# Two selective-scan layers and two token layers on one core: another order of the state loads, other transfers for B, C and delta, one more state buffer

## The chip, the cores and the metric

The kernel runs on one core of a Trainium2 chip. The metric is device time in microseconds; lower is better. Three runs of the kernel before gave 12473.74, 12483.95 and 12504.42 us; their median, 12483.95 us, is what the change is compared with.

## The reference

The input is a batch of four 64 x 64 images with 96 channels. Layers 0 and 1 normalise the image and add the result of a two-dimensional selective scan; layers 2 and 3 are token layers (an attention without softmax and a quantised feed-forward block). The change touches the scan layers alone. In these an image is projected to 192 channels (E), convolved, and read in four directions (K): by rows, by columns, and both backwards. Each direction gives sequences of L = 4096 steps. Cut to what matters:

```python
dts, Bmat, Cmat = split(x_dbl, [R, R + N])          # R = 6, N = 16 states
delta = softplus(dts @ dt_w + bias)                 # per direction and channel
A = -exp(A_logs)
def step(h, inp):                                   # h: batch, direction, channel, 16 states
    u, d, b, c = inp
    h = exp(d * A) * h + d * b * u
    y = sum over the states of h * c
```

So every channel of every direction and image has 16 states that run through 4096 steps. The four directions' y are added, normalised, gated and projected.

## The kernel before

Two images are worked on together, so there are four phases: layer 0 for pairs 0 and 1, layer 1 for pairs 0 and 1 (`Scans.run`). Each phase has a preparation (`prepare`), which writes what the scan needs to DRAM, and a scan stretch (`scan_phase`), followed by a finish that runs beside the next preparation. Last come the token layers.

The 128 partitions of the scan are 4 groups of states (a "quarter" of 32 partitions each) x 8 sequences (G: 4 directions x 2 images) x 4 states. The time axis is cut into 8 chunks (NC) of 512 steps (TC), the channels into 16 blocks (NEB) of 12 (EB). A block of a chunk is a unit; a stretch has 128 units, four stretches 512.

Preparation writes four things to DRAM per chunk: delta, split into three bf16 parts that add up to the fp32 value (NP16 = 3, L323); the product du = delta x u twice, as two copies (L319); and the rows of B and C, 32 for each sequence (bc, L301).

For a unit, SyncE's queue gets these transfers, in the order of `store` and `load`:

- four stores of y of the unit before (L461),
- one load of delta, 24 partitions (3 parts x 8 sequences) of 12 channels x 512 steps in bf16, 12 KB a partition (L376),
- six loads of h, the state tile [128, 12, 512] in fp32, which starts out as du (L396). All 16 states of a sequence start from the same du, so a row of du is read four times for four partitions of a quarter. The two middle quarters (partitions 32 to 95) come by one transfer out of both copies, once for channels 0 to 5 and once for 6 to 11; then quarter 0 (partitions 0 to 31) in two transfers, then quarter 3 (96 to 127) in two.

B and C of a chunk are tiles of 128 partitions; each is loaded by four transfers of 32 partitions (L344). B of the next chunk is asked for after the last scan of block 8, C of the chunk after next after block 15.

On the chip a unit then passes through five engines, in an order written out by hand in `scan_phase`: POOL multiplies h by B in place, three channels at a time (L406); PE replicates delta onto the 128 partitions, adding up its three parts on the way, by a matmul with a 0/1 matrix `rep` on 24 rows (L412); ACT makes exp(A x delta) of it (L416); DVE runs the scan over 512 steps, one instruction per channel (L423); PE contracts the unit before with C over the states (L441), and ACT copies the result out (L453). The weights for the contraction, `cw`, are made by ACT from C (L360), 16 operations for a chunk: the first chunk's ahead of the first decay, the next chunk's in between, from block 2 on.

PE replicates four channels ahead of the scan, ACT decays three ahead, POOL is half a unit ahead. Units 0 to 2 are loaded at the start, with C of chunk 1 behind them; after the last scan of unit `at` the load of unit `at + 3` is issued. h has four buffers, delta three. Every transfer signals one of eight semaphores in turn and waits for the one that used that semaphore before it.

Of the kernel before, what the change touches and what calls it, by code (L numbers as in the profile page):

```python
# [9 lines left out]
F32 = mybir.dt.float32  # L10
F16 = mybir.dt.float16
BF16 = mybir.dt.bfloat16
# [12 lines left out]
NS = 16  # L25
R = 6
K = 4
G = 2 * K
PAD = HW + 2
TC = 512  # L30
NC = L // TC
ROWS = TC // HW
EB = 12
NEB = E // EB
ER = EB // 4
PITCH = 2
NP16 = 3
XD = 2 * NS + R + 1
XD2 = 64 + XD
HID = 384  # L40
# [40 lines left out]
class Consts:  # L81
# [9 lines left out]
        self.eps = pool.tile([128, 1], F32, name="eps")  # L91
        self.nc.vector.memset(self.eps, EPS)

    def scans(self, pool):
        rep = self.load(pool, "rep", [128, 128])
        self.rep = pool.tile([128, 128], BF16, name="rep16")
        self.nc.vector.tensor_copy(self.rep, rep)
        self.perm = self.load(pool, "perm", [128, K, 128])
        self.unit = self.load(pool, "unit", [128, 128])
        self.gmask = self.load(pool, "gmask", [128, G])  # L100
        self.group = self.load(pool, "group", [C, C])
        self.one_row = self.load(pool, "one_row", [XD2, 1])
# [25 lines left out]
class Scans:  # L128
    def __init__(self, tc, ctx, cst, a):
        nc = self.nc = tc.nc  # L130
        self.tc, self.cst, self.a = tc, cst, a

        def pool(name, bufs, **space):
            return ctx.enter_context(tc.tile_pool(name=name, bufs=bufs, **space))

        self.dram = pool("stage", 2, space=DRAM)
        self.keep = pool("keep", 2)
        cst.scans(pool("const_s", 1))

    def bank(self):  # L140
        return self.p_c.tile([128, TC], F32, name="c")
# [6 lines left out]
    def prepare(self, ph):  # L148

        nc, cst, a, pre = self.nc, self.cst, self.a, ph.pre  # L150
        ph.gs = self.keep.tile([C, 2, 2], F32, name="gs", bufs=3)
        ph.delta = [
            self.dram.tile([NP16, G, E, TC], BF16, name="delta", bufs=2 * NC) for _ in range(NC)
        ]


        ph.du = [
            self.dram.tile([2, G, E + PITCH, TC], F32, name="du", bufs=2 * NC) for _ in range(NC)
        ]
        ph.bc = [self.dram.tile([G, 2 * NS, TC], F32, name="bc", bufs=2 * NC) for _ in range(NC)]  # L160
        ph.ud = self.dram.tile([C, 2, HW, 2, 64], F32, name="ud")
        ph.y = self.dram.tile([64, G, 2, 2, NEB, 16 * EB], F32, name="y")
        x = ph.x_in[ph.pair]

        with self.tc.tile_pool(name="prep", bufs=1) as wp, self.tc.tile_pool(
            name="steps", bufs=2
        ) as sp:

            def load(name, shape, at=0):
                t = wp.tile([at + shape[0]] + shape[1:], F32, name=name)  # L170
                nc.sync.dma_start(t[at:], a[pre + name])
                return t

            xp = load("x_proj", [C, 2, 2, XD2])
            dt_w = load("dt_w", [XD2 - 2 * NS, 2, E], at=2 * NS)
            conv_b = load("conv_b", [C, 2])
            ds = load("Ds", [C, 2, K])
            dsum = wp.tile([C, 2], F32, name="dsum")
            nc.vector.tensor_reduce(dsum, ds, mybir.AxisListType.X, ALU.add)
            yield  # L180


            st = wp.tile([C, 2, 8, 6], F32, name="st")
            with self.tc.tile_pool(name="stats", bufs=2) as rp:
                for hl in range(8):
                    raw = rp.tile([C, 8, 2, 64], F32, name="raw")
                    nc.sync.dma_start(raw, x[:, hl * 8 : hl * 8 + 8])
                    for i in range(2):
                        nc.vector.bn_stats(st[:, i, hl], raw[:, :, i])
                    yield  # L190
            for i in range(2):
                mv = wp.tile([C, 2], F32, name="mv")
                nc.vector.bn_aggr(mv, st[:, i].rearrange("p c s -> p (c s)"))
                ps = self.bank()
                nc.tensor.matmul(ps[:C, :1], cst.group, mv[:, 0:1], start=True, stop=True)
                gs = ph.gs[:, i]
                nc.vector.tensor_copy(gs[:, 0:1], ps[:C, :1])
                d = wp.tile([C, 1], F32, name="d")
                nc.vector.tensor_tensor(d, mv[:, 0:1], gs[:, 0:1], ALU.subtract)
                nc.vector.scalar_tensor_tensor(d, d, d, mv[:, 1:2], ALU.mult, ALU.add)  # L200
                ps = self.bank()
                nc.tensor.matmul(ps[:C, :1], cst.group, d, start=True, stop=True)
                ln = wp.tile([C, 2], F32, name="ln")
                neg_rsqrt(nc, cst, ps[:C, :1], ln[:, 0:1], gs[:, 1:2], ln[:, 1:2])
                nc.vector.tensor_scalar_mul(gs[:, 1:2], gs[:, 1:2], -1.0)
                yield
            in_w = wp.tile([C, E], F32, name="in_w")
            nc.sync.dma_start(in_w, a[pre + "in_proj_w"][:, :E])
            taps = wp.tile([C, 9, E], F32, name="taps")
            nc.sync.dma_start(taps, a[pre + "conv_w"].unsqueeze(0).broadcast_to([C, 9, E]))  # L210

            nc.vector.tensor_tensor(
                taps, taps, in_w.unsqueeze(1).broadcast_to([C, 9, E]), ALU.mult
            )

            xc = [wp.tile([C, 2, L], F32, name="xc", bufs=2) for _ in range(2)]
            yield from self.convolve(ph, 0, x, xc[0], taps, conv_b, dsum)
            ph.beside = 0.5
            other = self.convolve(ph, 1, x, xc[1], taps, conv_b, dsum)
            for i in range(2):  # L220
                for c in range(NC):
                    for k in range(2):
                        yield from self.steps(ph, sp, xc[i], xp, dt_w, i, k, c)
                        for _ in range(2):
                            next(other, None)
                            yield
                for _ in other:
                    yield
                ph.beside = 1.7
# [52 lines left out]
    def steps(self, ph, sp, xc, xp, dt_w, i, k, c):  # L282


        nc, cst = self.nc, self.cst
        u = scan_view(xc, k, c)
# [3 lines left out]
        xd = sp.tile([XD2, TC], F32, name="xd")  # L290
# [7 lines left out]
        for back in range(2):  # L298
            at = 64 * back
            g, cc = 2 * (k + 2 * back) + i, NC - 1 - c if back else c  # L300
            nc.scalar.dma_start(ph.bc[cc][g], xd[at : at + 2 * NS])  # L301
            both.append((g, cc, scan_view(xc, k + 2 * back, cc), self.p_d.tile([C, 2, TC], F32, name="d")))
        for m in range(2):
            for back, (_, _, _, ps) in enumerate(both):
# [33 lines left out]
        ph.carry = self.keep.tile([128, E], F32, name="carry")  # L338
        ph.b, ph.c, ph.cw = {}, {}, {}

    def load_states(self, t, of):

        for a in range(4):
            self.nc.sync.dma_start(t[32 * a : 32 * a + 32], of[:, 4 * a : 4 * a + 4])  # L344

    def load_b(self, ph, c):
        ph.b[c] = self.units.tile([128, TC], F32, name="b")
        self.load_states(ph.b[c], ph.bc[c][:, :NS])

    def load_c(self, ph, c):  # L350
        ph.c[c] = self.units.tile([128, TC], F32, name="c")
        self.load_states(ph.c[c], ph.bc[c][:, NS:])

    def weights(self, ph, c, op):

# [15 lines left out]
    def load_delta(self, u):  # L371

        nc, ph = self.nc, u.ph
        u.dl = self.units.tile([NP16 * G, EB, TC], BF16, name="dlt", bufs=3)
        at = u.eb * EB
        nc.sync.dma_start(  # L376
            u.dl.rearrange("p e t -> p (e t)"),
            ph.delta[u.c][:, :, at : at + EB].rearrange("n g e t -> g n (e t)"),
        )

    def load(self, u):

        nc, ph = self.nc, u.ph
        u.h = self.units.tile([128, EB, TC], F32, name="h", bufs=4)
        self.load_delta(u)
        n = EB // 2
        for first, quarters in ((1, 2), (0, 1), (3, 1)):
            for e in range(0, EB, n):
                self.load_quarters(u, e, n, first, quarters)

# [17 lines left out]
    def replicate(self, u, n):  # L408

        u.a[n] = self.p_a.tile([128, TC], F32, name="a")  # L410
        rep = self.cst.rep[: NP16 * G]
        self.nc.tensor.matmul(u.a[n], rep, u.dl[:, n], start=True, stop=True)  # L412

    def decay(self, u, n):
        at = u.eb * EB + n
# [50 lines left out]
    def scan_phase(self, ph):  # L466
# [17 lines left out]
        with self.tc.tile_pool(name="units", bufs=2) as self.units, self.tc.tile_pool(  # L484
            name="p_a", bufs=6, space=PSUM
        ) as self.p_a, self.tc.tile_pool(name="p_y", bufs=2, space=PSUM) as self.p_y:
            with self.tc.manual_schedule():
# [3 lines left out]
                self.load_c(ph, 0)  # L491
                self.load(units[1])
                self.load(units[2])
                self.load_c(ph, 1)
                for t in range(-B_LEAD, 0, ER):
                    b_at(t)
# [6 lines left out]
                for at, u in enumerate(units):  # L503
                    before = units[at - 1] if at else None
                    for n in range(EB):
# [20 lines left out]
                        if n == EB - 1:  # L526
# [3 lines left out]
                                self.load_b(ph, u.c + 1)  # L530
                            if u.eb == NEB - 1 and u.c + 2 < NC:
                                self.load_c(ph, u.c + 2)
                            if at + 3 < last:
                                self.load(units[at + 3])
                for q in range(4):
                    self.contract(units[-1], q, 0)
                    self.contract(units[-1], q, 1)
# [364 lines left out]
def constants():  # L902

    p = np.arange(128)
    q = np.arange(C)
    rep = (p[:, None] % 32 < NP16 * G) & (p[:, None] % 32 // NP16 == p[None, :] // 4 % G)
    gmask = p[:, None] // 4 % G == np.arange(G)[None, :]


# [74 lines left out]
```

## Time and profile before

| | |
|---|---|
| median of three runs | 12483.95 us |
| the profiled execution's own time | 12443.48 us |
| its span | 12441.7 us |
| PE, DVE, POOL, ACT busy | 10107.0, 9376.9, 7386.0, 7185.6 us |
| mean granted TensorE clock | 0.665 |
| queue of SyncE and ACT's loads and stores (q1), share of 16 DMA engines | 50.6% |
| four scan stretches, first to last scan | 1909.5, 1910.9, 1912.1, 1928.4 us |
| preparations and finishes between them | 929 to 938 us each |

The times come from one profiled execution on the chip, whose time is 0.3% below the median. The page gives each engine's busy time, the span in 40 slices with busy shares in tenths, the chain of work that ended last, and groups of instructions: line, engine, operation, out<-in, shape, count, then busy us, mean ns of one, and the idle time before them with what ended most of it. "SPq" is SyncE's queue, which only issues transfers. A wait is put down to what came last. The timeline lists instructions in order of time. The windows view gives, for a stretch, its length, the busy time of PE, PE's weight loads, DVE, ACT and POOL with the number of instructions in brackets, then the granted clock, the DMA share and GB/s. Beside these views the trace holds a record of each DMA packet (queue, start, duration, size, but not the engine) and of each step of a semaphore by a DMA.

### The profile page before, as it was taken

Reading aid. Unit: us, or ns where it says so; the run is one execution under the profiler, and the core shown is the slowest. Engines: PE = TensorE matmul, PEld = TensorE weight load, DVE = VectorE, ACT = ScalarE, POOL = GpSimd, SP = SyncE. Lnnn points to the kernel's source line nnn. Section 1 sums busy time; section 2 is a strip of 40 time slices with the busy share of each in tenths; the row PEclk is TensorE's granted clock in tenths of the full one; section 3 lists DMA queues with packets and bytes.
Section 4 is the critical chain, followed back from the end, with each engine's and each line's share of the span. In section 5 each row is a group of like instructions: output and inputs, shape, how many; then the busy total and the mean of one; then the engine's idle time right before and its main releaser. Section 6 shows DMA issues by size and latency. Waiting matters only on the chain.

```text
span 12441.7 us, 340858 instructions
## 1 busy us (share of the span) xinstructions
PE 10107.0 (81%) x147008; PEld 4972.1 (40%) x147008; DVE 9376.9 (75%) x9235; ACT 7185.6 (58%) x11815; POOL 7386.0 (59%) x2316
## 2 busy tenths in 40 slices
PE   7758888879878888879878888888878888887777
PEld 2224444433334444433334444443334444444333
DVE  2479999963569999982469999992459999993567
ACT  2456666644456666653456666663446666662556
POOL 0159999950149998960139899880129989990000
PEclk8665565669675555659775656558776655557787
DMA  3567676754667676764566777664567666663110
GB/s 92 172 227 247 244 248 247 248 168 140 213 205 246 245 247 244 250 200 128 176 215 244 246 247 249 243 226 125 174 202 249 244 243 245 245 244 122 30 21 11
DMA packets 882704, 2491.45 MB, mean 200 GB/s; under 512 B 279058, under 2 KB 561840, under 8 KB 737456
## 3 DMA queue, kind: packets, MB, share of 16 engines
q1 hardware_dynamic: 552496, 2163.38, 50.6%
q10 hardware_dynamic: 328704, 306.26, 8.5%
q8 instruction: 1158, 18.97, 0.7%
q14 instruction: 346, 2.83, 0.1%
HBM read 1955.42 MB, written 513.80 MB: 198 GB/s over the span
## 4 chain that ended last, share of the span: by engine, by line
DMA 53%; PE 20%; SPq 8%; DVE 7%; ACT 4%; issue 4%; POOL 3%; ACTq 1%; POOLq 0%; DVEq 0%
DMA h<-du 47%; PE c L260 8%; SPq L396 7%; POOL h L406 3%; PE f L591 2%; DVE h L423 2%; PE d L306 2%; DMA yk<-y 1%; PE c L289 1%; PE f L600 1%; POOL parts L320 1%; PE f L682 1%; DMA du<-du_sb 1%; PE y L441 1%; DVE parts L321 1%
## 5 line engine op out<-in xcount | busy, mean ns | idle before, releaser
L406 POOL TENSOR_TENSOR h<-h,b 128x1536 f32<-128x1536 f32 x2048 | 7016.6, 3456 | 780.6 <-DMA h<-du 369.0
L423 DVE TENSOR_TENSOR_SCAN h<-a,carry,h 128x512 f32<-128x512 f32 x5376 | 6356.7, 1259 | 391.8 <-POOL h L406 360.9
L416 ACT ACTIVATE a<-a,a_col 128x512 f32<-128x512 f32 x6144 | 4030.3, 662 | 1966.6 <-PE a L412 1814.4
L441 PEld LDWEIGHTS y<-h,cw 128*32 128x32 f32 x131072 | 2886.3, 145 | 3597.6 <-issue 1606.1
L441 PE MATMUL y<-h,cw 128*32 128x48 f32 x131072 | 3702.1, 269 | 438.0 <-ACT a L416 216.9
L412 PE MATMUL a<-dlt,rep 24*128 24x512 bf16 x6144 | 3319.4, 551 | 884.8 <-DVE h L423 782.1
L320 POOL CAST parts<-dl 96x1024 bf16<-96x1024 f32 x256 | 341.3, 1348 | 3092.1 <-DVE dl L317 2785.6
L316 DVE TENSOR_TENSOR du_sb<-dl,xc 96x1024 f32<-96x1024 f32 x256 | 397.3, 1577 | 1296.2 <-ACT dl L314 1234.8
L453 ACT COPY d<-y 128x384 f32<-128x384 f32 x2048 | 979.6, 478 | 485.7 <-PE y L441 432.7
L260 PE MATMUL c<-xn,taps 96*96 96x512 f32 x2304 | 1034.1, 609 | 73.5 <-DVE xn L245 71.0
L423 DVE TENSOR_TENSOR_SCAN h<-a,h 128x512 f32<-128x512 f32 x768 | 869.6, 1201 | 189.0 <-ACT a L416 110.6
L412 PEld LDWEIGHTS <-rep 24*128 24x128 bf16 x6144 | 471.9, 101 | 903.6 <-issue 451.0
L306 PE MATMUL d<-xd,dt_w 7*96 7x512 f32 x1024 | 520.8, 859 | 254.9 <-ACT xd L292 225.6
L260 PEld LDWEIGHTS c<-xn,taps 96*96 96x96 f32 x2304 | 382.6, 167 | 707.5 <-issue 628.7
L823 POOL MEMSET tn<- 1x4096 f32 x8 | 27.8, 3506 | 865.0 <-PE pa L843 514.7
L267 ACT ACTIVATE xc<-c,conv_b 96x512 f32<-96x512 f32 x128 | 87.3, 682 | 718.1 <-PE c L260 633.2
L591 PE MATMUL f<-yk,perm 128*128 128x384 f32 x1024 | 415.9, 546 | 99.6 <-DMA yk<-y 88.8
L314 ACT ACTIVATE dl<-d 96x1024 f32<-96x1024 f32 x256 | 252.0, 1017 | 400.9 <-DMA delta<-parts 234.5
L321 DVE TENSOR_TENSOR parts<-dl,parts 96x1024 bf16<-96x1024 f32 x256 | 366.9, 1455 | 153.2 <-POOL parts L320 153.1
L289 PE MATMUL c<-xc,x_proj 96*103 96x512 f32 x512 | 420.2, 958 | 4.2 <-ACT xc L267 4.2
L306 PEld LDWEIGHTS d<-xd,dt_w 7*96 7x96 f32 x1024 | 151.7, 212 | 542.4 <-ACT xd L292 295.8
L360 ACT ACTIVATE cw<-c,gmask 128x256 f32<-128x256 f32 x512 | 287.9, 573 | 126.2 <-DMA h<-du 65.9
(114 smaller groups left out, 5650.6 us busy)
## 6 DMA issues: line engine op xcount, KB each, us to landing
h<-du SPq DMA_DIRECT2D x1024, 768.0 KB
h<-du SPq DMA_DIRECT2D x2048, 384.0 KB
delta<-parts ACTq DMA_DIRECT2D x512, 288.0 KB
dlt<-delta SPq DMA_DIRECT2D x512, 288.0 KB
du<-du_sb SPq DMA_DIRECT2D x256, 384.0 KB
du<-du_sb ACTq DMA_DIRECT2D x256, 384.0 KB
y<-d SPq DMA_DIRECT2D x2048, 48.0 KB
yk<-y SPq DMA_DIRECT2D x256, 384.0 KB
```

The costliest lines, as they stand in the source:

```text
L260: nc.tensor.matmul(rows(ps[:C]), taps[:, tap, h * C : (h + 1) * C], xn[:, ROWS * c + dy : ROWS * (c + 1) + dy, dx : dx + HW], start=tap == ...
L289: nc.tensor.matmul(rows(ps[:XD2]), xp[:, k, h], u[:, h], start=h == 0, stop=h == 1)
L306: nc.tensor.matmul(ps[:, m], dt_w[part, k, m * C : (m + 1) * C], xd[part], start=True, stop=True)
L321: nc.vector.tensor_tensor(parts[:, 2], delta, parts[:, 1], ALU.subtract)
L396: self.nc.sync.dma_start(u.h[32 * first : 32 * (first + quarters), e : e + n].rearrange("p e t -> p (e t)"), source.rearrange("a g e t -> ...
L406: self.nc.gpsimd.tensor_tensor(h, h, b, ALU.mult)
L412: self.nc.tensor.matmul(u.a[n], rep, u.dl[:, n], start=True, stop=True)
L416: self.nc.scalar.activation(u.a[n], u.a[n], AF.Exp, scale=u.ph.a_col[:, at : at + 1])
L423: self.nc.vector.tensor_tensor_scan(u.h[:, n], u.a.pop(n), u.h[:, n], 0.0 if u.c == 0 else u.ph.carry[:, at : at + 1], ALU.mult, ALU.add,)
L441: self.nc.tensor.matmul(view(u.y[32 * j : 32 * j + 32], l2 * EB, (8 * EB, 4), (1, EB)), u.ph.cw[u.c][:, l1, 8 * j + l2], view(u.h, 64 * l1 ...
L453: self.nc.scalar.copy(u.d[:, :, :, l1], u.y[:, : 32 * EB].rearrange("p (t h x) -> p t h x", t=4, h=2))
L591: nc.tensor.matmul(ps[:, : 4 * C].rearrange("p (w v e) -> p w v e", w=4, v=nv), cst.perm[:, k], view(t, off, (sw if k < 2 else -sw, 4), (1 ...
```

## The change

Four things change in the scan layers.

1. The order of the quarter loads of h: the middle quarters first as before, then quarter 3, then quarter 0.
2. bc in DRAM is laid out as [8, G, 4, TC], so that B and C of a chunk each lie in the order of the 128 partitions; each is loaded by one transfer of 128 partitions in place of four of 32. The store from preparation now writes 8 pieces of 4 rows.
3. A unit's delta is laid on 72 partitions (24 rows x 3 thirds of the block) of 4 channels x 512 steps, 4 KB each, in place of 24 partitions of 12 KB. The replication matrix has three versions, one for each third; each is zero on the rows of the other two, and the matmul runs over 72 rows in place of 24. Delta has four buffers.
4. h has five buffers; units 0 to 3 are loaded at the start, and after unit `at` the load of unit `at + 4` is issued.

The order of the instructions on PE, DVE, ACT and POOL is as before.

```diff
+DROWS = 3 * NP16 * G
+DC = EB // 3
...
-    def scans(self, pool):
-        rep = self.load(pool, "rep", [128, 128])
-        self.rep = pool.tile([128, 128], BF16, name="rep16")
-        self.nc.vector.tensor_copy(self.rep, rep)
+    def scans(self, tc, pool):
+        self.rep = pool.tile([DROWS, EB // DC, 128], BF16, name="rep16")
+        with tc.tile_pool(name="rep_f", bufs=1) as once:
+            rep = self.load(once, "rep", [DROWS, EB // DC, 128])
+            self.nc.vector.tensor_copy(self.rep, rep)
...
-        ph.bc = [self.dram.tile([G, 2 * NS, TC], F32, name="bc", bufs=2 * NC) for _ in range(NC)]
+        ph.bc = [self.dram.tile([NS // 2, G, 4, TC], F32, name="bc", bufs=2 * NC) for _ in range(NC)]
...
-            nc.scalar.dma_start(ph.bc[cc][g], xd[at : at + 2 * NS])
+            nc.scalar.dma_start(ph.bc[cc][:, g], xd[at : at + 2 * NS])
...
-    def load_states(self, t, of):
-        for a in range(4):
-            self.nc.sync.dma_start(t[32 * a : 32 * a + 32], of[:, 4 * a : 4 * a + 4])
+    def load_states(self, ph, c, first, name):
+        t = self.units.tile([128, TC], F32, name=name)
+        of = ph.bc[c][first : first + NS // 4]
+        self.nc.sync.dma_start(t, of.rearrange("a g s t -> (a g s) t"))
+        return t
...
-        u.dl = self.units.tile([NP16 * G, EB, TC], BF16, name="dlt", bufs=3)
+        u.dl = self.units.tile([DROWS, DC, TC], BF16, name="dlt", bufs=4)
...
-            ph.delta[u.c][:, :, at : at + EB].rearrange("n g e t -> g n (e t)"),
+            ph.delta[u.c][:, :, at : at + EB].rearrange(
+                "n g (h e) t -> (n g) h (e t)", h=EB // DC
+            ),
...
-        u.h = self.units.tile([128, EB, TC], F32, name="h", bufs=4)
+        u.h = self.units.tile([128, EB, TC], F32, name="h", bufs=5)
...
-        for first, quarters in ((1, 2), (0, 1), (3, 1)):
+        for first, quarters in ((1, 2), (3, 1), (0, 1)):
...
-        rep = self.cst.rep[: NP16 * G]
-        self.nc.tensor.matmul(u.a[n], rep, u.dl[:, n], start=True, stop=True)
+        h, e = divmod(n, DC)
+        self.nc.tensor.matmul(u.a[n], self.cst.rep[:, h], u.dl[:, e], start=True, stop=True)
...
                 self.load(units[2])
+                self.load(units[3])
                 self.load_c(ph, 1)
...
-                            if at + 3 < last:
-                                self.load(units[at + 3])
+                            if at + 4 < last:
+                                self.load(units[at + 4])
...
-    rep = (p[:, None] % 32 < NP16 * G) & (p[:, None] % 32 // NP16 == p[None, :] // 4 % G)
+    r = np.arange(DROWS)[:, None, None]
+    third = np.arange(EB // DC)[None, :, None]
+    rep = (r % 3 == third) & (r // 3 % G == p[None, None, :] // 4 % G)
```

More of the change, by code (lines that the diff above doesn't have):

```diff
@@ L137, in __init__ @@
         self.keep = pool("keep", 2)
-        cst.scans(pool("const_s", 1))
+        cst.scans(tc, pool("const_s", 1))
     def bank(self):
@@ L339, in start_phase @@
         ph.b, ph.c, ph.cw = {}, {}, {}
-    def load_states(self, t, of):
-        for a in range(4):
-            self.nc.sync.dma_start(t[32 * a : 32 * a + 32], of[:, 4 * a : 4 * a + 4])
+    def load_states(self, ph, c, first, name):
[3 more added lines that the diff above has]
+        return t
     def load_b(self, ph, c):
-        ph.b[c] = self.units.tile([128, TC], F32, name="b")
-        self.load_states(ph.b[c], ph.bc[c][:, :NS])
+        ph.b[c] = self.load_states(ph, c, 0, "b")
     def load_c(self, ph, c):
-        ph.c[c] = self.units.tile([128, TC], F32, name="c")
-        self.load_states(ph.c[c], ph.bc[c][:, NS:])
+        ph.c[c] = self.load_states(ph, c, NS // 4, "c")
     def weights(self, ph, c, op):
```

## The prediction

> **What bounds the kernel now.** I read the page first: busy rows, slices, chain, groups.
>
> ```profile
> DMA  3567676754667676764566777664567666663110
> ...
> DMA h<-du 47%; PE c L260 8%; SPq L396 7%; POOL h L406 3%; PE f L591 2%; DVE h L423 2%; PE d L306 2%; DMA yk<-y 1%; PE c L289 1%; PE f L600 1%; POOL parts L320 1%; PE f L682 1%; DMA du<-du_sb 1%; PE y L441 1%; DVE parts L321 1%
> ...
> L406 POOL TENSOR_TENSOR h<-h,b 128x1536 f32<-128x1536 f32 x2048 | 7016.6, 3456 | 780.6 <-DMA h<-du 369.0
> L423 DVE TENSOR_TENSOR_SCAN h<-a,carry,h 128x512 f32<-128x512 f32 x5376 | 6356.7, 1259 | 391.8 <-POOL h L406 360.9
> ```
>
> The chain lies for 47% on the loads of h and for 7% on their issue, in the four scan stretches. Yet DMA is only 7 tenths busy. POOL waits for those loads (369.0 us), DVE for POOL (360.9).
>
> Second, the timeline of DVE alone in one stretch: start, length, the idle time before it in brackets. One unit is 12 scans.
>
> ```profile
> 1351.23 14.21 DVE L423 TENSOR_TENSOR_SCAN h<-a,carry,h 128x512 f32<-128x512 f32 x12 [0.87 <-POOL h L406]
> 1366.19 14.21 DVE L423 TENSOR_TENSOR_SCAN h<-a,carry,h 128x512 f32<-128x512 f32 x12 [0.75 <-POOL h L406]
> 1381.08 14.21 DVE L423 TENSOR_TENSOR_SCAN h<-a,carry,h 128x512 f32<-128x512 f32 x12 [0.68 <-POOL h L406]
> 1396.39 14.21 DVE L423 TENSOR_TENSOR_SCAN h<-a,carry,h 128x512 f32<-128x512 f32 x12 [1.10 <-POOL h L406]
> 1414.45 14.21 DVE L423 TENSOR_TENSOR_SCAN h<-a,carry,h 128x512 f32<-128x512 f32 x12 [3.85 <-POOL h L406]
> 1428.93 42.45 DVE L423 TENSOR_TENSOR_SCAN h<-a,carry,h 128x512 f32<-128x512 f32 x36 [0.28 <-POOL h L406]
> ```
>
> Starts lie about 14.9 us apart; three units without a gap take 42.45, so DVE, PE and POOL can all hold 14.15. The 3.85 us stop recurs: by the starts of all 512 units, a unit takes 14.74 us on average, but two units in each chunk (eb 10 and eb 1, two units after the loads of B and C) take 17.53. From first to last scan the stretches last 1909.5, 1910.9, 1912.1 and 1928.4 us, 7660.9 in sum; the scans are busy 6356.7 + 869.6 = 7226.3. **So 434.6 us is all that any faster supply can give here.**
>
> Third, the chain in one unit, and SyncE's own waits:
>
> ```profile
> 1306.69 0.67 SPq L396
> ...
> 1308.09 12.54 DMA h<-du
> ...
> 1320.64 0.69 SPq L396
> ```
>
> ```profile
> SPq L396 <- DMA h<-du: 2039.9, 1326, 4.0
> ```
>
> SyncE issues quarters, the last lands 12.5 us later, only then does it issue again. Is that latency a queue of data or a shortage of transfers in flight? The packet records decide. From 1100 to 1600 us at least 8 packets are in flight 95% of the time, and exactly 8 or 9 half of it. A 12 KB packet takes 465 ns in the median, 550 in the mean. This looks like eight engines never idle and eight idle half the time.
>
> [...] So the halves (16 and 64 rows) use 16 engines; quarters (8 source rows), delta (8), B and C (8 each) use engines 0 to 7. [...] when the half of the next unit [...] starts while engines 0 to 7 still write quarter 3 [...], its first packets take 1.3 to 1.8 us; those at a stretch's start, without such a neighbour, mostly 0.56 to 0.85. [...]
>
> **Engines 0 to 7, per unit, before:** 8 packets of halves, 16 of quarters, 3 of delta: 27 x 465 ns = 12.56 us. Stores of y: 16 x 36 ns = 0.58. The rest of 14.74, 1.6 us, is slowed packets.
>
> **The change, part by part.**
> *Delta on 72 partitions.* 24 source rows and 72 target rows give 12 engines: six 4 KB packets each, not three of 12 KB. Records show 84 ns for 2 KB and 460 for 12 KB, so 4 KB is about 0.16 us (bounds: 0.153 by proportion, 0.23 with the slow tail). 3 x 0.465 - 6 x 0.16 = 0.435 us per unit, x 512 = 223 us while engines 0 to 7 bind; at 0.23 nothing. The matmul keeps 512 columns and its weights 128; L412's 551 ns I leave (K=128 takes 546 for 384 columns, so rows may cost up to some 0.18 us each; PE is discussed below).
> *B and C by one transfer.* 128 rows on both sides: 16 engines, 8 packets of 2 KB (0.67 us) in place of 16 (1.34), and one issue of 0.66 us for four. Of the excess 17.53 - 14.74 = 2.79 us I leave 0.9 (bounds 0.67 and 1.33). In a stretch 13 loads show it (7 B, 6 C): 1.9 x 13 x 4 = 99 us. The store of bc falls from 16 engines to 8: two more 84 ns packets, in preparation, where PE and ACT end last: nothing; without that cover 0.2 us x 256 = 43.
> *Start of a stretch.* C of chunk 0 lands some 3 us earlier (three issues fewer and no lane waits); 16 cw operations of 573 ns and the first scan hang on it: -4 us a stretch, -16 (bounds 0 and -20). Unit 3's load now stands on SyncE's queue ahead of C of chunk 1; ACT's cw at unit 2 waits for that, decays queue behind it, DVE's three decays in hand cover 3.5 us: +1 a stretch (bounds 0 and 4).
> *Order of quarters.* The same transfers; [...] Worth 0 to 0.9 of the 1.6 us. I take 0.4.
> *Five buffers.* Depth yields no bandwidth; it only absorbs stops. Costs nothing: 120 + 16 KB a partition in place of 96 + 36. SyncE still issues behind the y stores, at the same point of a unit. Delta's fourth buffer is free by then (PE replicates four ahead, so unit `at` has been replicated after scan 7, the load for `at` + 4 is issued after scan 11). Once SyncE is no longer late, it waits at h for PE's last contraction of unit `at` - 1, after scan 10; behind it stand only that load's other parts and the next y stores, due 12 scans later: nobody waits for them.
> *rep constant.* x_proj now waits for its copy: under 2 us, once.
>
> **Sum.** Supply per unit: 14.74 - 0.435 - 0.4 = 13.9 us, below DVE's 14.12. So the next bound is DVE, with POOL (4 x 3.456 = 13.8) just under it. Of 434.6 us idle I leave 18 a stretch (10 units of chunk 0, where DVE's starts lie 13.38 apart while data lasts, against 13.9: 5; C of chunk 1: 1; jitter: 12): 434.6 - 72 + 16 = 379. Against the profiled execution's 12,443.5 us that is 12,065; against the median, 12,484, which lies 0.3% higher, **12,105**.
>
> **Rivals.**
> 1. *Engines 0 to 7 still bind* (order worth nothing): 14.3 per unit; 223 + 99 + 8 = 330 saved, 12,154. [...]
> 2. *Delta's small packets cost what they save*: 99 + 16, order a little: 12,350. For it: slow packets' mean is 550, not 465. Against: 2 KB at 84 ns.
> 3. *Slower: delta lands on fewer engines than 12.* Place: the front of each unit's loads. At 8 engines nine packets, 1.44 us, equal the 1.40 removed; below that it loses. At 4: 2.88 us, +1.5 x 512 = 768, less 115: 13,140. [...]
> 4. *PE becomes the bound*: at clock 0.50 it is busy 12.54 of 14.10 us, as below, so 12 replications may each grow by 0.13 us before it decides; at 0.18, +0.05 x 12 x 512 = 307 goes back: near 12,410.
>
> ```profile
> 1306.70:1320.80 14.10, 12.54 (x240) 5.86 (x236) 14.10 (x12) 9.74 (x17) 12.95 (x4) 0.50 0.70 256
> ```
>
> **Numbers.** DVE bound 0.55; rival 1 0.25; rival 2 0.10; rival 4 0.06 (half of it, with a growth a little over 0.18 us, within 0.3%); rival 3 0.04. Measurement tells 0.3% (37 us) from no change. Faster 0.93, same 0.03, slower 0.04. The range runs from all idle time gone (12,484 - 454 = 12,030) to between rivals 1 and 2, 12,270.
>
> **What would show it.** DVE gaps per stretch fall from 104 to about 20 and units stand at 14.12; the stops at eb 1 and 10 vanish; loads of h fall from the chain and DVE scans lead it; first packets of halves under 1 us. Wrong if delta's packets exceed 0.23 us, if units stay at 14.7, or if L412 exceeds 0.7 us.

## The result and the profile after

The changed kernel takes 12,296.97 us (median, 12,285.55 to 12,306.23) against 12,488.62 of the kernel before beside it: ratio 0.9846, 95% interval 0.9829 to 0.9863. It gains 1.5%, about 190 us, where 379 were forecast. All ratios below are against the kernel before as it ran in the same measurement (medians of 12,455 to 12,504 us). The two profiled executions lie 137 us apart, because that of the kernel before was below its median. The profiled execution has a span of 12,304.4 us. Of the page of the changed kernel: the DMA row of the slices, the chain by line, the groups of POOL and DVE:

```profile
DMA  3577777754667777764567777764567777773110
...
DMA h<-du 51%; SPq L401 8%; PE c L263 8%; PE f L597 2%; PE d L309 2%; DMA yk<-y 1%; PE c L292 1%; DMA delta<-parts 1%; PE f L606 1%; POOL parts L323 1%; DMA du<-du_sb 1%; PE f L688 1%; PE f L677 1%; DVE parts L324 1%; PE f L663 1%
...
L411 POOL TENSOR_TENSOR h<-h,b 128x1536 f32<-128x1536 f32 x2048 | 7020.1, 3462 | 626.3 <-DMA h<-du 237.2
L428 DVE TENSOR_TENSOR_SCAN h<-a,carry,h 128x512 f32<-128x512 f32 x5376 | 6347.3, 1259 | 241.6 <-POOL h L411 238.3
```

The loads of h have not left the chain, they grew from 47% to 51%. DVE's idle time ahead of the scans fell from 391.8 to 241.6 us, but it still ends with POOL, and POOL's with h. DVE in the middle of the first stretch:

```profile
1346.74 42.42 DVE L428 TENSOR_TENSOR_SCAN h<-a,carry,h 128x512 f32<-128x512 f32 x36 [1.83 <-POOL h L411]
1389.83 14.21 DVE L428 TENSOR_TENSOR_SCAN h<-a,carry,h 128x512 f32<-128x512 f32 x12 [0.67 <-POOL h L411]
1405.48 14.21 DVE L428 TENSOR_TENSOR_SCAN h<-a,carry,h 128x512 f32<-128x512 f32 x12 [1.44 <-POOL h L411]
1420.95 42.41 DVE L428 TENSOR_TENSOR_SCAN h<-a,carry,h 128x512 f32<-128x512 f32 x36 [1.26 <-POOL h L411]
1463.85 14.21 DVE L428 TENSOR_TENSOR_SCAN h<-a,carry,h 128x512 f32<-128x512 f32 x12 [0.48 <-POOL h L411]
```

The stops near 3.85 us are gone: by the starts of the units those at eb 1 and 10 stand at 14.27 and 14.16 us (17.55 and 17.48 before). The others stand at 14.76, before at 14.74 (the prediction's average is of these): no change. The four stretches last 1,883.9, 1,875.6, 1,879.8 and 1,875.6 us, 7,514.8 in sum, 146 less than before. The preparations and finishes between them take 933 to 944 us, as before. SyncE's wait for the loads of h has grown from 2,039.9 us:

```profile
SPq L401 <- DMA h<-du: 2382.1, 1455, 3.9
```

Where did the gain on delta go? The trace holds each step of a transfer's semaphore by a DMA. Before, each of the 2048 quarters, the 512 loads of delta and the 256 of B and C gives 9 steps, each half and each store of y 16; in the changed kernel a load of delta gives 13, one of B or C 16, and the rest is as before. I read this as 8, 12 and 16 engines, with one step more wherever it is not all 16. Steps and packets name no engine: "engines 0 to 7" stands for the eight of a transfer of 9 steps, "8 to 15" for the others. That it is always the same eight is an estimate, from 8 or 9 packets in flight for half of the time from 1100 to 1600 us before.

I take the slowest step of each transfer and its distance from the slowest of the transfer ahead: how long the slowest of engines 0 to 7 is held up, per transfer, averaged from 1000 to 2500 us. (B and C have a column of their own; "quarters in order" are the four quarter transfers of a unit in the order of issue.)

```
us per unit     y     delta  half 1 half 2  quarters in order        B,C    sum
before          1.11  1.77   1.68   1.96    1.87 1.92 1.88 2.69      0.19   15.1
after           1.07  1.03   1.76   2.03    1.86 1.88 2.62 2.47      0.03   14.8
```

Delta gives 0.74 us, more than the 0.435 forecast. The last two transfers, now both of quarter 0, take 0.52 back. Quarter 3 did get what the prediction hoped for: its two transfers take 1.86 and 1.88 us in place of 1.88 and 2.69. But quarter 0 in its place takes 2.62 and 2.47. Why is the question for the experiments.

### The profile page after: what moved, and what is told of

The parts are those of the page before. It is cut to its first block, busy times and chain, and to the rows that moved or that the text cites. A ratio compares the mean times of both kernels' runs of the same rounds, so it can differ in the third digit from the quotient of the medians.

```text
span 12304.4 us, 340148 instructions
## 1 busy us (share of the span) xinstructions
PE 9373.2 (76%) x147008; PEld 4896.4 (40%) x147008; DVE 9361.4 (76%) x9235; ACT 7057.5 (57%) x11815; POOL 7390.8 (60%) x2316
## 4 chain that ended last, share of the span: by engine, by line
DMA 57%; PE 19%; SPq 9%; DVE 5%; ACT 4%; issue 3%; POOL 1%; ACTq 1%; DVEq 0%; POOLq 0%
DMA h<-du 51%; SPq L401 8%; PE c L263 8%; PE f L597 2%; PE d L309 2%; DMA yk<-y 1%; PE c L292 1%; DMA delta<-parts 1%; PE f L606 1%; POOL parts L323 1%; DMA du<-du_sb 1%; PE f L688 1%; PE f L677 1%; DVE parts L324 1%; PE f L663 1%
## 5 line engine op out<-in xcount | busy, mean ns | idle before, releaser
L428 DVE TENSOR_TENSOR_SCAN h<-a,carry,h 128x512 f32<-128x512 f32 x5376 | 6347.3, 1259 | 241.6 <-POOL h L411 238.3
L446 PEld LDWEIGHTS y<-h,cw 128*32 128x32 f32 x131072 | 2789.0, 129 | 3551.2 <-issue 1349.3
L417 PE MATMUL a<-dlt,rep 72*128 72x512 bf16 x6144 | 2539.6, 424 | 1333.5 <-DVE h L428 1247.9
L417 PEld LDWEIGHTS <-rep 72*128 72x128 bf16 x6144 | 487.3, 99 | 883.4 <-issue 640.4
```

What stands on the lines that cost most here:

```text
L417: self.nc.tensor.matmul(u.a[n], self.cst.rep[:, h], u.dl[:, e], start=True, stop=True)
L428: self.nc.vector.tensor_tensor_scan(u.h[:, n], u.a.pop(n), u.h[:, n], 0.0 if u.c == 0 else u.ph.carry[:, at : at + 1], ALU.mult, ALU.add,)
L446: self.nc.tensor.matmul(view(u.y[32 * j : 32 * j + 32], l2 * EB, (8 * EB, 4), (1, EB)), u.ph.cw[u.c][:, l1, 8 * j + l2], view(u.h, 64 * l1 ...
```

## Experiments

My theory after the result: engines 0 to 7 still bind, and what the new order was to relieve it makes worse. In the expectations "ports theory" is the name of my guess that quarter 3 and the next unit's halves slow each other by the partitions that they write, and "the ports of delta" are its partitions; that ports are behind it was not shown. Rivals: the five buffers or the start of a stretch cost something; the copy of du that is read matters; DVE and the supply stop each other in turn.

**The parts alone.** Three kernels are the kernel before with one part each.

```diff
 e1: +  ph.bc = [NS // 2, G, 4, TC] in DRAM; load_states: one transfer of 128 partitions
 e2: +  u.dl = [DROWS, DC, TC], bufs=3; rep of three thirds; matmul over 72 rows
 e3: -  for first, quarters in ((1, 2), (0, 1), (3, 1)):
     +  for first, quarters in ((1, 2), (3, 1), (0, 1)):
```

> The kernel before with B and C by one transfer each, and nothing else of the change. Theory 1 (the gain of the change is that the stops at blocks 1 and 10 are gone, and little else): 13 stops of 2.8 us in each of four stretches fall to under 1 us, so 100 to 150 us faster than before, and units without such a load stay at 14.7 us. Theory 2 (the gain comes from delta on 12 engines): 30 us or less.

> The kernel before with delta on 72 partitions alone (three delta buffers, four buffers of h). Theory 1: a unit's other transfers take up what delta frees, 14.6 to 14.75 us for a unit without a load of B or C, so 0 to 70 us faster. Theory 2: 14.3 us or less for such a unit, 200 us faster or more. The matmul on 72 rows: if the warm clock in the changed kernel comes from the 72 rows, the mean clock rises from 0.67 to about 0.85 here too; if it comes from the other edits, it stays.

> The kernel before with quarter 3 ahead of quarter 0 and nothing else. Ports theory [...]: 0.4 us a unit less, 200 us faster, and the last quarter no longer stretched. Load theory (any transfer of engines 0 to 7 is slowed while engines 8 to 15 also load, whatever the partitions): no change within 0.3%, the last quarter again near 2.7 us against 1.85.

Measured: B and C 0.9965 (0.9952 to 0.9979), some 44 us; delta 0.9893 (0.9876 to 0.9911), 134 us; the order 1.0176 (1.0156 to 1.0197), a loss of 220 us. The sum would be a loss of 42; together, with the fifth buffer (which e6 below shows to be worth nothing), they gain 190. So the parts act on each other. By the semaphore steps the order alone (e3) leaves quarter 3 at 1.86 and 1.89 us, but quarter 0 behind it takes 2.34 and 2.71, and delta 1.98 in place of 1.77. In e1 the stops go, but the units without a stop grow to 15.10 us: I take it that part of each stop was work that the engines now do evenly spread.

**The changed kernel less one part.**

```diff
 e5: -  ((1, 2), (3, 1), (0, 1))    +  ((1, 2), (0, 1), (3, 1))
 e4:    self.load_c(ph, 1) ahead of self.load(units[3])
 e6:    h bufs=4, dlt bufs=3, loads three units ahead
 e9: -  slice(first % 2, first % 2 + 1)   +  slice(1 - first % 2, 2 - first % 2)
```

> The changed kernel with the old order of the quarters (0, then 3). Load theory: the two last transfers of a unit are stretched as in the changed kernel, whichever quarter they fill, and the time is that of the changed kernel within 0.3%. Ports theory: 100 to 200 us slower than the changed kernel. Reverse (the new order costs): 50 us or more faster.

> The changed kernel with C of chunk 1 loaded ahead of unit 3, as in the kernel before. If the stop of 12 us at unit 2 of each stretch is a loss: 30 to 48 us faster than the changed kernel, so 0.980 to 0.982 of before. If the transfers go on during the stop and the scan catches up from the full buffers (the supply binds, not the scan): 0 to 10 us faster than the changed kernel.

> The changed kernel with four buffers of h, three of delta and loads three units ahead. If depth is worth nothing where supply binds: the same within 0.3% but for the stop at unit 2 of a stretch, which goes. If the fifth buffer absorbs the stops that are left: 50 us or more slower.

> The changed kernel (quarter 0 last) with the two copies of du in DRAM swapped for the quarters: quarter 0 reads copy 1, quarter 3 copy 0. The partitions written stay. If the new order costs because of what is read (the last quarter now reads copy 0): the time of the changed kernel with the old order, 0.978 of before. If it costs because of the partitions that are written: that of the changed kernel, 0.984.

Measured: without the new order 0.9783 (0.9762 to 0.9804), 12,224.6 us, so the order costs 70 to 80 us here too. The three others stand with the changed kernel: C of chunk 1 early 0.9832 (0.9817 to 0.9847), four buffers 0.984 (0.9824 to 0.9855), the other copy of du 0.9841 (0.9827 to 0.9855). Buffers, the start and the copy read are not the cause.

The start of a stretch is worth a line, since a stop there costs nothing. DVE, ACT and SyncE's queue in the changed kernel at the first stretch's unit 2:

```profile
817.26 23.51 DVE L428 TENSOR_TENSOR_SCAN h<-a,h 128x512 f32<-128x512 f32 x21 [11.97 <-ACT a L421]
```

```profile
816.12 0.56 ACT L363 ACTIVATE cw<-c,gmask 128x256 f32<-128x256 f32 x1 [16.38 <-DMA c<-bc]
```

```profile
797.82 0.33 SPq L348 DMA_DIRECT2D c<-bc  x1
```

C of chunk 1 is asked for at 797.82, behind unit 3's load; ACT waits 16.38 us for it in front of its decays, and DVE stands for 11.97. In e4 that stop is 2.11 us, yet the time is the same within the intervals: during the stop the loads go on, and the units behind it run faster from what has piled up. The first chunk's units take 14.53 us in the mean with the stop and 14.43 without.

**Engines and partitions.** e7 loads all of h as quarters, by the reading above on engines 0 to 7 alone; e8 as halves of 64 partitions, 0 to 63 and 64 to 127, on 16 engines each.

```diff
 e7: +  for first, quarters in ((1, 1), (2, 1), (3, 1), (0, 1)):
 e8: +  for first, quarters in ((0, 2), (2, 2)):
```

> The changed kernel with the two middle quarters loaded one by one as well, so that all loads of h run on engines 0 to 7 and engines 8 to 15 do next to nothing. It measures the slowing by itself. Load theory: each of eight quarter transfers takes 1.85 us with none stretched, 14.8 + 1.0 (delta) + 1.1 (y) = 16.9 us a unit, about 900 to 1100 us slower than before. If engines 0 to 7 are slow by themselves [...]: the last transfers are stretched here too, 18 us a unit or more, over 1500 us slower.

> The changed kernel with h loaded by two halves (partitions 0 to 63, then 64 to 127) on 16 engines each, four transfers for six, no quarters. The share of engines 0 to 7 falls from 24 packets of 12 KB to 16. If engines 0 to 7 bind by their count of packets: DVE becomes the bound, 14.15 us a unit, 350 to 450 us faster than before. If the ports bind[...]: packets of 12 KB take about 0.9 us with all 16 engines on one half, 14.7 us for 256 packets and 16 us or more a unit, 500 us slower than before or worse.

e7: 1.1227 (1.1207 to 1.1247). With no halves on engines 8 to 15, far fewer packets are slow: from 1000 to 2500 us 3.6 packets of 12 KB a unit take over 1 us, against 12.5 in the changed kernel. By the semaphore steps the first six quarters of a unit take 1.67 to 1.96 us in the mean. But the last two, both of quarter 0, take 2.48 each, much as in the changed kernel (2.62 and 2.47). So the loss on quarter 0 does not need the halves beside it. A unit takes 18.1 us, not the 16.9 of the load theory; of the two expectations the numbers of the second were met. e8: 1.1068 (1.1049 to 1.1087), though all 16 engines share all of h. The queues of e8, then the same row of the changed kernel (packets, MB, share of 16 engines):

```profile
q1 hardware_dynamic: 578036, 2163.43, 70.5%
```

```profile
q1 hardware_dynamic: 578036, 2163.43, 52.6%
```

The same packets and bytes hold the engines for more of a longer span; a 12 KB packet takes 935 ns in the median, not 465. That is twice the time, where each transfer writes one half of the partitions. What holds the packets up was not shown.

**Delta on other partitions.** e11 is the kernel before with delta's 24 rows at partitions 96 to 119; e10 is that with the new order.

```diff
-  u.dl = [NP16 * G, EB, TC]
+  u.dl = [128, EB, TC], load and matmul on u.dl[96 : 96 + NP16 * G]
```

> The kernel before, old order, with delta's 24 rows on partitions 96 to 119. Neighbour theory: [...] the mirror of the new order, so 1.01 to 1.02. If the ports of delta don't matter: within 0.3% of before.

> The kernel before with quarter 3 ahead of quarter 0 (which took 1.018 of before) and with delta's 24 rows on partitions 96 to 119 in place of 0 to 23. Neighbour theory (quarter 0 is followed on the same engines by delta[...]): the cost of the order goes, 0.995 to 1.003. If the order costs by its own (quarter 0 against the next half): 1.012 to 1.02.

e11: 1.0629 (1.0611 to 1.0647); e10: 1.0205 (1.0189 to 1.0221). With delta high the new order is the better one by 4 points; with delta low (1 and 1.0176) the worse. That delta stood behind quarter 0, on the same low half, is thus not all that the order costs, but where delta lies decides over the order.

**Delta at another place in the queue.** e12, e16 and e17 are the changed kernel with load_delta moved; e15 is the kernel before, so treated. In signs (H the two halves, D delta on 72 rows, d on 24, 0 and 3 the transfers of quarters):

```diff
 before: d H 0 0 3 3       after:  D H 3 3 0 0      e5:  D H 0 0 3 3
-         self.load_delta(u)
         for first, quarters in ...:
             for e in range(0, EB, n):
                 self.load_quarters(u, e, n, first, quarters)
+                if first == 3 and e == 0:
+                    self.load_delta(u)
 e12: H 3 D 3 0 0          e16: H 0 D 0 3 3         e15: H 0 d 0 3 3
 e17: H 3 3 0 0 D
```

> The changed kernel with the load of delta issued between the two transfers of quarter 3, away from quarter 0. Neighbour theory: 0.4 us a unit or more less than the changed kernel, 0.965 to 0.976 of before, near what the scan allows (0.967). If the ports of delta don't matter: 0.98 to 0.987.

> The kernel before with one edit: delta is issued between the two transfers of quarter 0, not ahead of the halves of h; delta's shape, the order of quarters, B and C and the buffers stay. If delta's place acts by itself (the next unit's halves then wait for a landing with three transfers of a quarter or delta behind it, not two, so engines 8 to 15 start earlier), it gains 100 to 300 us: 12,190 to 12,390. If it needs the split of delta, because delta of 12 KB packets on engines 0 to 7 takes 1.77 us wherever it stands, it is within 60 us of the kernel before.

> The changed kernel with quarter 0 ahead of quarter 3, as before, and delta issued between the two transfers of quarter 0. If what counts is at which landing the next unit's halves are issued, the order of the quarters is indifferent now and it stands with the kernel that has delta between the transfers of quarter 3, at 12,010 us, within 40. If the order costs by the partitions that the quarters and the halves write at the same time, it differs from that by more than 60 us: faster is hidden by the scans, so it would show as slower.

> The changed kernel with delta issued last, behind both transfers of quarter 0. The next unit's halves are then issued when the second transfer of quarter 3 lands, and engines 8 to 15 run them beside quarter 0 and delta on engines 0 to 7. If what costs is that quarter 3 (partitions 96 to 127) is written beside halves that write 64 to 95, nothing of that is left here: units at 14.1 us, 12,000 to 12,060 us. If delta between the two transfers of quarter 3 was good by another accident of the order, this stays near the changed kernel, 12,250 to 12,320.

Measured: e12 0.9603 (0.9588 to 0.9618), 12,008.89 us, faster than both kernels; e16 1.0426 (1.041 to 1.0441); e15 1.0903 (1.0884 to 1.0922); e17 0.9752 (0.9738 to 0.9765). POOL and DVE in e12, then in e16:

```profile
L412 POOL TENSOR_TENSOR h<-h,b 128x1536 f32<-128x1536 f32 x2048 | 7021.0, 3474 | 308.8 <-DMA h<-du 153.5
L429 DVE TENSOR_TENSOR_SCAN h<-a,carry,h 128x512 f32<-128x512 f32 x5376 | 6320.5, 1255 | 13.0 <-POOL h L412 12.4
```

```profile
L412 POOL TENSOR_TENSOR h<-h,b 128x1536 f32<-128x1536 f32 x2048 | 7013.0, 3457 | 1304.8 <-DMA h<-du 422.6
L429 DVE TENSOR_TENSOR_SCAN h<-a,carry,h 128x512 f32<-128x512 f32 x5376 | 6365.5, 1261 | 858.3 <-POOL h L412 852.7
```

In e12 the scans wait 13.0 us, in e16 858.3. The two differ only in the order of the quarters, that is, in which one surrounds delta and comes first and which one is last, ahead of the next unit's halves: same transfers, sizes, engines and places in the turn of the eight semaphores. DVE in e12, where 110 scans run with no gap, and in e16, where nearly every unit has one:

```profile
1361.92 28.31 DVE L429 TENSOR_TENSOR_SCAN h<-a,carry,h 128x512 f32<-128x512 f32 x24 [0.42 <-POOL h L412]
1391.17 129.36 DVE L429 TENSOR_TENSOR_SCAN h<-a,carry,h 128x512 f32<-128x512 f32 x110 [0.94 <-POOL h L412]
```

```profile
1370.41 14.21 DVE L429 TENSOR_TENSOR_SCAN h<-a,carry,h 128x512 f32<-128x512 f32 x12 [1.47 <-POOL h L412]
1386.55 14.21 DVE L429 TENSOR_TENSOR_SCAN h<-a,carry,h 128x512 f32<-128x512 f32 x12 [1.93 <-POOL h L412]
1402.91 14.21 DVE L429 TENSOR_TENSOR_SCAN h<-a,carry,h 128x512 f32<-128x512 f32 x12 [2.16 <-POOL h L412]
```

My theory for e15 to e17 (the landing at which the next unit's halves are issued decides) fell: e16 has e12's landings and loses.

**The supply by itself.** In e13 (the changed kernel) and e14 (e12) each product with B and each scan takes only the first 256 of 512 steps, so that half of the recurrence is left out. PE and ACT keep their full work; the loads are unchanged.

```diff
-  h = u.h[:, ER * r : ER * r + ER]
+  h = u.h[:, ER * r : ER * r + ER, : TC // 2]
-  u.h[:, n], u.a.pop(n), u.h[:, n]
+  u.h[:, n, : TC // 2], u.a.pop(n)[:, : TC // 2], u.h[:, n, : TC // 2]
```

> The changed kernel with every product with B and every scan on only the first 256 of the 512 steps (the second half of the recurrence is left out), so that DVE and POOL need about 7 us for a unit and only the loads are left to set its length. If the supply is what bound the changed kernel, units stay near 14.8 us and the time near 12,290 us, because nothing of its loads is changed; a scan stretch then stays near 1,880 us. If DVE and the supply only take turns in stopping each other, units fall to 14.3 us or less and the time to 12,050 or less.

> The kernel with delta between the two transfers of quarter 3, with the same half of the recurrence left out. If delta's place makes the supply itself faster, units fall clearly below DVE's 14.12 us, to 13.2 to 13.8, and the time to 11,550 to 11,850 us. If its supply is only just as fast as the scans (engines 0 to 7 are busy without a gap at 14.13 us a unit in the run before), units stay at 14.0 to 14.15 and the time near 12,000.

e13: 0.9846 (0.983 to 0.9862); e14: 0.9547 (0.953 to 0.9564). The windows of e13 and of e14 (columns as in the view before):

```profile
1300.00:1400.00 100.00, 76.83 (x1836) 43.72 (x1835) 55.04 (x84) 66.61 (x124) 49.03 (x28) 0.83 0.74 253
```

```profile
1300.00:1400.00 100.00, 79.79 (x1918) 45.58 (x1921) 54.74 (x85) 71.53 (x131) 52.20 (x30) 0.85 0.76 272
```

DVE is busy 55 of 100 us and the changed kernel still takes its full time: units stand at 14.75 us, with whole scans at 14.76. PE and ACT are busy 77 and 67 of 100 us, and with the same work on them e14 is faster. So its pace is the supply's. With delta between, the supply runs at 13.94 us a unit, below DVE's 14.12.

**Both together.** e18 is e12 with C of chunk 1 early, as in e4.

> The kernel with delta between the two transfers of quarter 3, and C of chunk 1 loaded ahead of unit 3 at the start of a stretch. There the scans bind, so the stop of unit 2 (21.2 us where others take 14.1) is now paid: without it 7 us a stretch, 28 us in all, about 11,980 us. If the time is caught up from the buffers as it was in the changed kernel, it stays at 12,009 within 15.

12,000.42 us, 0.9603 (0.9589 to 0.9617). The four stretches fall from 7,229.0 to 7,215.9 us in the traces, but the total's interval is that of e12: 13 us, if they are there, are less than this measurement tells.

## Why the prediction was wrong

**The order of quarters: the step that failed.** "Worth 0 to 0.9 of the 1.6 us. I take 0.4." It was an estimate: that the time of a packet goes by the half of the partitions that it writes had not been shown. It has the other sign: alone it costs 220 us, 0.43 us a unit; in the changed kernel 70 to 80, about 0.15 a unit. So the supply of 13.9 us a unit, and with it the DVE bound, was not reached: units stayed at 14.76, which the text named as a sign of error, and e13 shows that this is the supply. A loss lay outside my bounds because I looked at one neighbour only, the halves of the next unit beside quarter 3, and not at what the new order puts ahead of delta.

How the slowdown goes with the neighbours I could see in part. I estimated from issue and landing when engines 8 to 15 work on the next unit's halves, and took the quarters that lie over 1 us beside that. Where these are of quarter 3 they take 3.27 us (e2), 3.17 (e5), 3.29 (e16) and 2.81 (before); where they are of quarter 0, 2.62 (after), 2.61 (e17), 2.94 (e3) and 1.95 (e12). For quarter 3 this fits the prediction, which had it collide with the halves: with none beside it (e7) it takes 1.87 and 1.96. For quarter 0 the halves are not the cause: without them it takes 2.48 us (e7), and beside them 1.95 where delta does not follow it (e12). In both it is the last of a unit, with y's stores behind it. In e7 delta comes next, in e12 the halves. That points to delta next to quarter 0, which I had not foreseen.

A reading that fits more, made after the runs and thus only argued: a delta in flight and other writes to its own half of the partitions hold each other up; on what they meet was not shown. In e12 it stands between transfers to the other half; in before, e2 and e5 one neighbour is in its half (the halves' lower part); in after and e3 both are (quarter 0 ahead, the halves behind); in e15 and e16 two quarters 0 surround it. With delta low and its shape the same, the times rise in just this order: e12, e5, after, e16 for 72 rows; before, e3, e15 for 24. e17, with quarter 0 ahead of delta and y's stores behind, is not placed by it; it came out a little better than e5. Nor does it place delta high: e10 and e11 (1.0205 and 1.0629) lie above before and e3 (1 and 1.0176), and in e10 the last transfer of quarter 0 still takes 2.53 us, though delta is then in the other half.

In the steps it is one engine that falls behind. In the last quarter of a unit the slowest engine lands 2.0 us after the next slowest in the changed kernel, 1.7 in e12 and 5.4 in e16 (medians). The records name no engine for a packet, so which engines collide, and on what, stays open. The untried test is a delta whose rows each engine writes on the partitions that it writes of a quarter.

**Delta split: the mechanism right, the size not.** Its packets: median 159 ns as estimated (0.16 us), mean 226. Per unit the slowest engine is held 0.74 us less by delta, against 0.435 forecast; but alone the part brought 134 us, not 223. In e2 the last quarter takes 3.11 us (2.69 before): the gain is partly lost to slower packets behind.

**B and C: mis-sized, 44 us for 99 + 16.** The stops vanished as said. I counted the whole excess of a stopped unit as a gain, while engines 0 to 7 bound all other units too: what a load really saves is 8 packets of 84 ns, 0.67 us; by 13 loads and four stretches that is 35 us, and 44 were measured (26 to 60 by the interval).

**C of chunk 1: mis-sized without harm.** The stop was 12 us, not 1; with the supply as bound, nothing is lost by it (e4), and hardly more with DVE as bound (e18).

**Five buffers: right.** e6 is the same.

**Rivals.** Rival 1's mechanism is what happened, with a price for the order on top: it gave 12,154 for an order worth nothing, and e5, which has the old order, took 12,224.6. The 70 us between them are about what B and C fell short by (44 for 115). Rival 2 fell with delta's packets, rival 3 with the semaphores: a load of delta steps its own 13 times, where it was 9: by the reading above 12 engines, where it was 8. Rival 4 went the other way: PE was busy for less of a unit. PE's windows of before were 12.54 us busy of 14.10; a unit of the changed kernel, and the replications:

```profile
1346.75:1360.85 14.10, 10.52 (x223) 5.19 (x211) 14.10 (x12) 9.45 (x18) 14.10 (x5) 0.76 0.77 236
```

```profile
L417 PE MATMUL a<-dlt,rep 72*128 72x512 bf16 x6144 | 2539.6, 424 | 1333.5 <-DVE h L428 1247.9
```

**The signs named.** Two came true in the changed kernel (the stops gone, delta's packets short) and L417 stayed under 0.7 us. Two more came true only in e12: few gaps (13.0 us), units at 14.13. That the loads of h leave the chain came true in neither: they hold 50% of it in e12 too. So the chain's shares did not tell which of two nearly equal bounds sets the pace; the gaps of DVE did. Its 12,009 us lies under the forecast, so the bound that I named exists; the change does not reach it.

## What to carry to other kernels

When several transfers share a queue and not all use every engine, their order can be a cost of its own: the same swap of quarters gained 8 points of the time (e12 against e16) or lost 2 (e3), by where a third, smaller transfer stood. So time the orders; the count of packets did not tell them apart. Parts of a change that feed the same bound do not add (alone the three came to a loss of 42 us, together to a gain of 190); price them on that bound. To learn whether the loads or the engines set the pace, halve the engines' work and leave the loads: if the time stays (e13, 0.9846 as before the halving), it is the loads.

## What the hardware showed unexpectedly

A replication takes 424 ns in the mean in the changed kernel and 551 before, and the mean granted clock of the two profiled executions is 0.849 and 0.665. It goes with delta's part: these lines of e2 (72 rows, clock 0.850) and e3 (24 rows, clock 0.763) stand against 561 ns at 0.651 in e1 (24 rows):

```profile
L417 PE MATMUL a<-dlt,rep 72*128 72x512 bf16 x6144 | 2554.3, 425 | 1450.3 <-DVE h L428 1343.4
...
L412 PE MATMUL a<-dlt,rep 24*128 24x512 bf16 x6144 | 2902.5, 479 | 1514.9 <-DVE h L423 1415.9
```

The length follows the clock, not the rows. Length times clock is 366 ns before and 365 in e1 and e3, with 24 rows; 360 in the changed kernel, 361 in e2 and 362 in e16 (446 ns at 0.811), with 72. Over all runs it lies at 357 to 370 with 24 rows and at 360 to 376 with 72, but at 390 in the slow e8. So within a few per cent 72 rows cost nothing by themselves.

The clock is less simple. In one measurement e2 ran at 0.847 to 0.850 in five executions, e1 at 0.651 to 0.786 and the kernel before at 0.649 to 0.785. That kernel has two levels at the same time: 12,506 us at 0.649, 12,483 to 12,527 us at 0.776 to 0.785. The clock thus did not set its time. Over all executions the kernels with 72 rows lie at 0.768 to 0.859, the lowest being the slow e7 and e8, those with 24 at 0.607 to 0.790. PE is busy for 81% of the span before and for 76% after, and the clock is higher after; but with a higher clock the busy time is also shorter (551 ns a replication at 0.665, 424 at 0.849), so this does not tell whether the clock depends on how busy PE is. Whether rows or the three alternating weights raise the clock, and what makes the two levels, was not tried.
